# A two-layer perceiver on one core: another order of the first transfers and the first norm, and a feed-forward with one set of transposes and a written-out order

## The chip, the core and the metric

The kernel runs on one core of a Trainium2 chip, everything in 32-bit floats. The metric is device time in microseconds. One core has five engines with a program each: TensorE (PE; its weight loads are listed as PEld), VectorE (DVE), ScalarE (ACT), GpSimd (POOL) and SyncE (SP), whose queue issues nearly all transfers here. Engines wait for one another through semaphores; each works through its own program in order.

## The reference

The state `x` is 4 x 256 tokens of 256 numbers, the context 4 x 4096 rows of 256. Two layers, each a cross attention, a second block and a feed-forward:

```
x = x + L0_xattn(layernorm(x), ctx)     # scores times values, softmax over the 64 features of a head:
                                        #   no softmax over the keys, so keys and values enter as a gram matrix
x = x + L0_attn(layernorm(x))           # relative-position attention over the 4 batch entries, 16 heads
x = x + L0_ffn(layernorm(x))            # below
x = x + L1_xattn(layernorm(x), ctx, mask)   # softmax attention over 4096 masked keys
x = L1 self attention with rope and relu FFN, then L1 attention with 8 gated experts

def L0_ffn(u):                          # u = layernorm(x)
    experts(u, g, W1, b1, W2, b2) = gelu((u * rsqrt(mean(u*u) + eps) * g) @ W1 + b1) @ W2 + b2
    shared = sum of experts 0..1 on every token            # hidden size 1024
    scores = sigmoid(u @ centroids)                         # 8 routed experts
    gates, chosen = top_2(scores);  gates = gates / scores.sum()
    routed = sum over the two chosen of gate * expert
    return u + shared + routed
```

So after the feed-forward `x` has become x + u + shared + routed.

## The kernel before

`build` makes the constants, loads `x`, and then runs the blocks `l0_xattn`, `l0_attn`, `l0_ffn`, and the second layer, which the change leaves alone. The tokens lie as 8 tiles of 128 (`TT` = 8); `DC` = 2 is the width in units of 128, `FF` = 1024 the hidden size, `FC` = 8 the hidden size in units of 128, `NE` = 8 the routed experts. A `pool` hands out memory: a tile with a tag and `bufs=n` takes one of n buffers in turn and waits until the buffer's last reader is done. PSUM has 8 banks of 128 x 512; `mm_tile` takes one of three, `sc_tile` one of four in the feed-forward (`sc=(4, 1)`), `ps_o` has one. `contract` issues the matmuls of one product. A matmul in 32-bit floats appears as two records in the trace.

**Order.** Outside of a `manual_schedule()` a scheduler orders the instructions of a block by their dependences and estimated costs. Inside, each engine runs its instructions in the order in which the program states them. `l0_xattn` is written out in that way; `l0_ffn` isn't, up to its routed tiles.

**The start.** `Net.__init__` issues on SP the constants `cols` and `consts` and the mask; DVE turns the mask into additive numbers, `added`, and SP writes them to `away` in DRAM, where the second layer reads them. Then come `x`, and in `l0_xattn` chunk 0 of the context. The context goes through a ring of 4 chunks of 1 MB (`fetch`, 8 row tiles each, 4 chunks per batch entry); POOL sets a column of ones in each ring tile. `products(b, first, last)` adds up the gram matrix of batch entry b over its row tiles (lines 414 and 415). The written order is `products(0, 0, KC)`, the norm of `x` (`normed`, DVE: statistics at 240 and 241, an inverse root in 12 small operations at 183 to 190, `xn` at 247), 16 transposes on PE (`transposed`, line 263), 64 query matmuls, and then the batch entries one after another.

**The feed-forward, `l0_ffn`**, in the order of its text:

1. `normed` gives `u`, and `ms`, its mean square. `transposed` makes `uT`; 8 products of it with the centroids (`cs`) give the logits (line 812).
2. `score`, `top2` and the sums that make `chosen` and `gates` (line 827 and before it).
3. POOL adds `u` to `x`, tile by tile; `u` is multiplied by the inverse root of `ms` (line 827), and transposed a second time, with the shared gain, into `sT`.
4. `place` works out for each token its row in the list of slots of the routed experts: a `rank` product on PE (707, 708), a row of small DVE operations, one POOL operation (`part`, line 765, 1472 elements in each partition) and a reduction of it on DVE (line 769). Then 16 indirect transfers (line 832) scatter the tokens to `f0_rows` in DRAM.
5. For each of the 8 token tiles: the gates are transposed (`gT`, 839), copied by ACT (841), multiplied with the second biases `f0_b2` (843), and added to `x` by DVE (844).
6. For each of the 2 shared experts and each of 4 blocks of 256 tokens: the hidden layer `h`, where each f of `FC` is a product of two matmuls into half a PSUM bank, followed by ACT's gelu (867); f = 0 and 1 share a bank, 2 and 3 the next one, and so on. Then, for two tiles, the product with `w2` (`eo`, line 175 as all products of `contract`) and the add to `x` (872).
7. 23 tiles of routed slots, with the weights of the 8 routed experts (16 MB, `w1_all`, `w2_all`), which are loaded from the end of the attention on.

The loop of item 6, whose products and gelus the scheduler orders:

```
for f in range(FC):
    if f % 2 == 0:
        sc = self.sc_tile("h")[:, 0, :]
    part = sc[:, f % 2 * 256 : (f % 2 + 1) * 256]
    self.contract(part, [(w1[:, k, f * P : (f + 1) * P], sT[:, k, cols]) for k in range(DC)])
    nc.scalar.activation(h[:, f, :], part, AF.Gelu, bias=self.col("f0_b1", (NE + e) * FC + f))
```

Of the kernel before, what the change touches and what calls it, by code (L numbers as in the profile page):

```python
# [11 lines left out]
F32 = mybir.dt.float32  # L12
U8 = mybir.dt.uint8
# [5 lines left out]
P = 128  # L19
# [55 lines left out]
class Net:  # L75
    def __init__(self, ctx, tc, a, out):
# [14 lines left out]
        nc.sync.dma_start(self.cols, a["cols"])  # L91
        nc.sync.dma_start(self.consts, a["consts"])
        self.ones = self.const.tile([1, P], F32, name="ones")
        nc.vector.memset(self.ones, 1.0)

        self.away = tc.dram_tile([B, NK], F32, name="away")
        with tc.tile_pool(name="mask", bufs=1) as first:
            masked = first.tile([P, B * KC], U8, name="masked")
            nc.sync.dma_start(masked, a["mask"])
            added = first.tile([P, B * KC], F32, name="added")  # L100
            nc.vector.tensor_copy(added, masked)
            nc.vector.tensor_scalar(added, added, MASKED, None, ALU.mult)
            nc.sync.dma_start(self.away.rearrange("b (p k) -> (b p) k", k=B * KC), added)
        self.all_ones = self.const.tile([P, P], F32, name="all_ones")
        nc.vector.memset(self.all_ones, 1.0)

# [126 lines left out]
    def normed(self, x, out, tiles=range(TT), square=None):  # L233

        nc = self.nc
        n = len(tiles)
        stats = self.small.tile([P, n, 6], F32, tag="bn", name=self.name("bn"))
        mv = self.small.tile([P, n, 2], F32, tag="mv", name=self.name("mv"))
        for k, i in enumerate(tiles):
            nc.vector.bn_stats(stats[:, k, :], x[:, i, :])  # L240
            nc.vector.bn_aggr(mv[:, k, :], stats[:, k, :])
        rstd = self.rsqrt(mv[:, :, 1], EPS)
        if square is not None:
            nc.vector.tensor_mul(square, rstd, rstd)
            nc.vector.tensor_mul(square, square, mv[:, :, 1])
        for k, i in enumerate(tiles):
            nc.vector.tensor_scalar(
                out[:, i, :], x[:, i, :], mv[:, k, 0:1], rstd[:, k : k + 1], ALU.subtract, ALU.mult
            )
        return out  # L250
# [108 lines left out]
    def l0_xattn(self, x):  # L359
# [7 lines left out]
        with ExitStack() as ctx:  # L367
# [13 lines left out]

            fetch(0)
            fetch(1)
            wq = self.load_w(pool, "x0_wqT")
            fetch(2)

            brow = pool.tile([64, 512], F32, name="x0_brow")
            for j in range(2):
                nc.sync.dma_start(
                    brow[32 * j : 32 * j + 32, :], a["x0_qb"][:, j * 512 : (j + 1) * 512].partition_broadcast(32)  # L390
                )
            wo = self.load_w(pool, "x0_woT")
            ob = self.row("x0_ob")
# [3 lines left out]
            nc.vector.tensor_scalar(fixed[0], brow, rank[:64, 2:3], None, ALU.mult)  # L397
            nc.vector.tensor_scalar(fixed[1], brow, rank[:64, 0:1], None, ALU.mult)
# [120 lines left out]
            with self.tc.manual_schedule():  # L519
                products(0, 0, KC)  # L520
                xn = self.normed(x, self.tokens("xn"))
                xT = self.transposed(xn, "xT")
# [23 lines left out]
    def l0_attn(self, x):  # L546
# [3 lines left out]
        with ExitStack() as ctx:  # L550
# [6 lines left out]
            nc.sync.dma_start(bias, a["a0_bias"].partition_broadcast(P))  # L557

# [212 lines left out]

    def l0_ffn(self, x):
# [4 lines left out]
        with ExitStack() as ctx:  # L777
            pool = self.block(ctx, "f0", sc=(4, 1))
            rows = self.tc.dram_tile([SLOT_TILES * P, D], F32, name="f0_rows")
            results = self.tc.dram_tile([SLOT_TILES * P, D], F32, name="f0_results")  # L780
            cent = self.load_w(pool, "f0_cent")
            b2 = self.load(pool, "f0_b2", [NE + 2, D], a["f0_b2"])
            zero = pool.tile([P, D], F32, name="f0_zero")
            nc.gpsimd.memset(zero, 0.0)
            nc.sync.dma_start(
                rows.rearrange("(t p) d -> p t d", p=P), zero.unsqueeze(1).to_broadcast([P, SLOT_TILES, D])
            )
# [3 lines left out]
            ms = self.small.tile([P, TT], F32, tag="ms", name=self.name("ms"))  # L791
            u = self.normed(x, self.tokens("xn"), square=ms)
            w1_all, w2_all = (pool.tile([P, NE, DC * FF], F32, name=f"f0_w{n}_all") for n in (1, 2))
            with self.tc.tile_pool(name="f0_shared", bufs=1, reuse_waits="tile") as first:
                weights = {}

                def shared_weights(e):
                    weights[e] = (
                        self.load(first, "w1", [P, DC, FF], a["f0_W1_s"][e].rearrange("(k p) n -> p k n", p=P)),
                        self.load(first, "w2", [P, FC, D], a["f0_W2_s"][e].rearrange("(k p) n -> p k n", p=P)),  # L800
                    )

                shared_weights(0)
                uT = self.transposed(u, "xT", pool=first)
                score = first.tile([P, TT, NE], F32, name="f0_score")
                ps = self.mm_tile("cs")
                for i in range(TT):
                    self.contract(
                        ps[:, i * NE : (i + 1) * NE], [(uT[:, k, i * P : (i + 1) * P], cent[:, k, :]) for k in range(DC)]
                    )  # L810
                logit = first.tile([P, TT, NE], F32, name="f0_logit")
                nc.vector.tensor_copy(logit, ps[:, : TT * NE].rearrange("p (t e) -> p t e", e=NE))

                nc.scalar.activation(score, logit, AF.Exp, scale=-1.0)
                nc.vector.tensor_scalar(score, score, 1.0, None, ALU.add)
                nc.vector.reciprocal(score, score)
                nc.vector.tensor_copy(chosen, self.top2(score, logit, first))
                total = self.small.tile([P, TT], F32, tag="total", name=self.name("total"))
                nc.vector.tensor_reduce(total, score, AX.X, ALU.add)
                nc.vector.reciprocal(total, total)  # L820
                nc.vector.tensor_mul(score, score, chosen)
                nc.vector.tensor_mul(gates[:, :, :NE], score, total.unsqueeze(2).to_broadcast([P, TT, NE]))

                r = self.rsqrt(ms, EPS_RMS)
                for i in range(TT):
                    nc.gpsimd.tensor_add(x[:, i, :], x[:, i, :], u[:, i, :])
                    nc.vector.tensor_scalar(u[:, i, :], u[:, i, :], r[:, i : i + 1], None, ALU.mult)
                sT = self.transposed(u, "xT", "f0_gs", pool=first)
                slots, shares, where, bias = self.place(first, pool, chosen, gates[:, :, :NE])
                for side in range(2):  # L830
                    for i in range(TT):
                        nc.gpsimd.indirect_dma_start(
                            out=rows, out_offset=bass.IndirectOffsetOnAxis(ap=slots[:, side, i : i + 1], axis=0),
                            in_=u[:, i, :], in_offset=None,
                        )

                for i in range(TT):
                    ps = self.mm_tile("gT")
                    nc.tensor.transpose(ps[: NE + 2, :P], gates[:, i, :], self.ident)
                    gT = self.small.tile([NE + 2, P], F32, tag="gT", name=self.name("gT"))  # L840
                    nc.scalar.copy(gT, ps[: NE + 2, :P])
                    ps = self.mm_tile("b2")
                    nc.tensor.matmul(ps[:, :D], gT, b2, start=True, stop=True)
                    nc.vector.tensor_add(x[:, i, :], ps[:, :D], x[:, i, :])
                for e in range(2):
                    if e:
                        shared_weights(e)
                    w1, w2 = weights[e]
                    if not e:
                        for r in range(NE):  # L850
                            nc.sync.dma_start(
                                w1_all[:, r, :].rearrange("p (k n) -> p k n", k=DC),
                                a["f0_W1_r"][r].rearrange("(k p) n -> p k n", p=P),
                            )
                            nc.sync.dma_start(
                                w2_all[:, r, :].rearrange("p (k n) -> p k n", k=FC),
                                a["f0_W2_r"][r].rearrange("(k p) n -> p k n", p=P),
                            )
                    for n in range(4):
                        cols = slice(n * 256, (n + 1) * 256)  # L860
                        h = first.tile([P, FC, 256], F32, tag="h", name=self.name("h"), bufs=2)
                        for f in range(FC):
                            if f % 2 == 0:
                                sc = self.sc_tile("h")[:, 0, :]
                            part = sc[:, f % 2 * 256 : (f % 2 + 1) * 256]
                            self.contract(part, [(w1[:, k, f * P : (f + 1) * P], sT[:, k, cols]) for k in range(DC)])
                            nc.scalar.activation(h[:, f, :], part, AF.Gelu, bias=self.col("f0_b1", (NE + e) * FC + f))
                        for q in range(2):
# [950 lines left out]
```

## Time and profile before

| | us |
|---|---|
| median of 3 runs | 2364.1 (2363.99 to 2373.08) |
| the profiled execution | 2370.56 |
| its span, first to last instruction | 2368.8 |
| PE busy in the span | 2224.3 (94%) |
| start to the first gram product | 14.3 |
| norm of `x` in `l0_xattn`, PE idle | 8.1 |
| last `x` add of the attention to the first routed layer | 360.7 to 511.3 |
| second layer | from about 700 on |

Times in the trace count from the start of the span. "PEclk" is the share of full speed that TensorE was granted; at 0.5 a matmul takes twice as long. A line "A <- B: total, times, longest" says that A waited for B.

### The profile page before, as it was taken

What the parts mean: (1) busy time and instruction counts of PE and PEld (TensorE: products, weight loads), DVE (VectorE), ACT (ScalarE), POOL (GpSimd) and SP (SyncE); (2) the same over time, 40 slices, a digit from 0 to 9 for tenths busy, and PEclk for the clock granted to TensorE, in tenths of its full rate; (3) what the DMA queues carried; (4) which work ended last, traced back from release to release, by engine and by line L of the source; (5) the groups of instructions that cost most, each with busy time, mean ns of one, the idle gap of its engine ahead of it and who ended that gap; (6) DMA issues with size and microseconds to landing.
All of it is one profiled execution on the core that took longest, in us unless ns stands there. A gap on an engine that the chain in (4) does not pass through costs nothing.

```text
span 2368.8 us, 45856 instructions
## 1 busy us (share of the span) xinstructions
PE 2224.3 (94%) x19148; PEld 1339.5 (57%) x19148; DVE 1189.0 (50%) x2494; ACT 982.6 (41%) x1942; POOL 146.5 (6%) x270
## 2 busy tenths in 40 slices
PE   6999877999988999999999999999999899999996
PEld 4677535876752454455545554455554566666552
DVE  2333476012215766666666666665665176343545
ACT  0111111223333366655666556655555524344321
POOL 0000002100011000000000000000000042000121
PEclk9999866999999999999999999999999999999977
DMA  6121118101124112211121112210000120000000
GB/s 202 54 89 32 36 51 293 63 16 36 32 87 147 45 39 66 66 31 35 49 64 56 32 34 61 63 46 29 29 7 2 62 78 1 1 1 1 6 0 14
DMA packets 82432, 121.50 MB, mean 51 GB/s; under 512 B 5466, under 2 KB 52338, under 8 KB 82226
## 3 DMA queue, kind: packets, MB, share of 16 engines
q1 hardware_dynamic: 80690, 114.38, 15.4%
q0 software_dynamic: 1536, 4.20, 0.5%
q8 instruction: 151, 2.47, 0.4%
q14 instruction: 55, 0.45, 0.1%
HBM read 109.32 MB, written 9.24 MB: 50 GB/s over the span
## 4 chain that ended last, share of the span: by engine, by line
PE 87%; DVE 6%; issue 3%; ACT 2%; DMA 2%; SPq 0%; POOL 0%; POOLq 0%; DVEq 0%; ACTq 0%
PE sc L1092 14%; PE acc L1143 10%; PE mx L1105 9%; PE h L175 8%; PE v L1000 5%; PE k L1000 5%; PE ro L175 4%; PE we L175 3%; PE gram L414 2%; PE eo L175 2%; PE po L175 2%; PE sc L1560 2%; PE q L175 2%; PE xo L175 1%; PE qkv L175 1%
## 5 line engine op out<-in xcount | busy, mean ns | idle before, releaser
L1134 DVE TENSOR_REDUCE mx<-mx 128x1 f32<-128x512 f32 x988 | 636.6, 686 | 365.0 <-PE mx L1105 361.0
L1130 ACT ACTIVATE probs<-sc 128x512 f32<-128x512 f32 x988 | 536.8, 597 | 422.2 <-PE mx L1105 394.9
L1092 PE MATMUL sc<-qm,kT 32*128 32x256 f32 x3952 | 581.3, 401 | 8.9 <-ACT probs L1130 8.9
L1105 PE MATMUL mx<-kT,x_q 32*128 32x512 f32 x1976 | 561.1, 639 | 0.0
L1092 PEld LDWEIGHTS sc<-qm,kT 32*128 32x128 f32 x3952 | 352.3, 184 | 255.0 <-ACT probs L1130 129.3
L1143 PE MATMUL acc<-probs,v 128*32 128x256 f32 x4096 | 275.6, 386 | 0.0
L1143 PEld LDWEIGHTS acc<-probs,v 128*32 128x32 f32 x4096 | 107.3, 109 | 134.9 <-issue 90.1
L1105 PEld LDWEIGHTS mx<-kT,x_q 32*128 32x128 f32 x1976 | 150.9, 183 | 8.5 <-issue 7.2
L1000 PE MATMUL k<-slab,x_wk 128*32 128x512 f32 x1024 | 136.1, 618 | 11.8 <-DMA slab<-in_ctxT 10.9
L1000 PE MATMUL v<-x_wv,slab 128*32 128x256 f32 x2048 | 137.1, 385 | 0.0
L1574 DVE TENSOR_REDUCE negm<-mx 128x2 f32<-128x512 f32 x128 | 82.7, 686 | 94.8 <-PE mx L1566 92.9
L1572 ACT ACTIVATE probs<-sc 128x512 f32<-128x512 f32 x128 | 69.5, 595 | 136.1 <-PE mx L1566 93.9
L1566 PE MATMUL mx<-k,q 32*128 32x256 f32 x512 | 90.3, 435 | 24.5 <-DVE negm L1574 19.5
L309 ACT ACTIVATE kT<-k,cols 128x512 f32<-128x512 f32 x128 | 92.8, 783 | 23.2 <-PE k L1000 23.2
L346 POOL COPY wide<-rec 128x256 f32<-128x256 f32 x48 | 19.1, 398 | 1328.4 <-DVE rec L344 1317.0
L1000 PEld LDWEIGHTS v<-x_wv,slab 128*32 128x32 f32 x2048 | 53.4, 109 | 74.4 <-issue 46.3
L414 PE MATMUL gram<-x_ctx 128*128 128x257 f32 x256 | 79.2, 391 | 14.3 <-DMA x_ctx<-in_ctx 14.3
L1560 PE MATMUL sc<-qm,k 32*128 32x256 f32 x512 | 88.6, 439 | 0.0
L175 PE MATMUL h<-f_w_all,rT 128*128 x184 | 83.0, 594 | 0.7 <-DVE rT L888 0.6
L175 PE MATMUL ro<-f_w_all,hT 128*128 x368 | 83.3, 379 | 0.1
L912 ACT ACTIVATE hT<-hT,place 128x128 f32<-128x128 f32 x184 | 49.9, 383 | 77.8 <-PE hT L909 77.7
L175 PEld LDWEIGHTS ro<-f_w_all,hT 128*128 128x128 f32 x368 | 68.2, 190 | 9.1 <-issue 0.5
(365 smaller groups left out, 2664.4 us busy)
## 6 DMA issues: line engine op xcount, KB each, us to landing
slab<-in_ctxT SPq DMA_DIRECT2D x96, 512.0 KB
x_ctx<-in_ctx SPq DMA_DIRECT2D x16, 1024.0 KB
f_w_all<-in_f_W_r SPq DMA_DIRECT2D x16, 1024.0 KB
w<-in_f_W_s SPq DMA_DIRECT2D x4, 1024.0 KB
f_rows<-f_zero SPq DMA_DIRECT2D x1, 2944.0 KB
row<-f_rows SPq DMA_DIRECT2D x23, 128.0 KB
f_results<-y SPq DMA_DIRECT2D x23, 128.0 KB
kT<-away SPq DMA_DIRECT2D x128, 8.0 KB
```

What stands on the lines that cost most here:

```text
L175: nc.tensor.matmul(out, w, m, start=i == 0, stop=i == len(pairs) - 1)
L309: nc.scalar.activation(dst, ps, AF.Identity, bias=b, scale=own)
L414: nc.tensor.matmul(ps[:, : D + 1], t[:, :P], t, start=n == 0, stop=False)
L1000: nc.tensor.matmul(out[own], w[:, own], m, start=start, stop=not start, tile_position=(0, 32 * j))
L1092: nc.tensor.matmul(into[:, c * S : (c + 1) * S], kT[b, u, at // HALF][rows, at % HALF : at % HALF + P], qm[un][rows, :], start=True, stop= ...
L1105: nc.tensor.matmul(into, q[rows, b, u, t * P : (t + 1) * P], kT[b, u, at // HALF][rows, at % HALF : at % HALF + SLAB], start=True, stop=True,)
L1130: nc.scalar.activation(probs[j], sc[j], AF.Exp, scale=0.25)
L1134: nc.vector.tensor_reduce(mx[un2][:, k2 % 2, j, k2 // 2 : k2 // 2 + 1], bd[j], AX.X, ALU.max)
L1143: nc.tensor.matmul(acc[32 * j : 32 * j + 32, :S], v[b, chunk // VC][:, at : at + 32], probs[j][:, c * S : (c + 1) * S], start=k == 0 and c ...
L1560: nc.tensor.matmul(sc[j][:, c * S : (c + 1) * S], k[key][on_rows(j), u, c * P : (c + 1) * P], qm[i][on_rows(j), :], start=True, stop=True,)
L1566: nc.tensor.matmul(bd[j][:, c * S : (c + 1) * S], q[key][on_rows(j), u, c * P : (c + 1) * P], k[key][on_rows(j), u, :], start=True, stop=True,
L1574: nc.vector.tensor_reduce(negm[i2 % 2][:, :, 32 * j + UNIT_MAX[i2 % 2]], bd[j].rearrange("p (t s) -> p t s", s=S), AX.X, ALU.max, negate=True,
```

## The change

Three parts in one kernel.

1. **Start.** SP issues chunk 0 of the context first, then `x`, chunk 1, `cols`, `consts`, chunk 2 and `wq`. The norm stands in front of the first products; after a quarter of those, the text issues `brow`, `wo`, `ob` and the mask with its conversion (now a method, `mask`). The transposes follow the products as they did.
2. **Early loads.** A pool that lives through attention and feed-forward holds a zero tile, the centroids, `f0_b2`, and the first shared expert's `w1` and `w2`; `before_ffn` issues them and the filling of `f0_rows` with zeros (2944 KB) behind the attention's own weights.
3. **Feed-forward.** `u` is brought to its second scale at once (`by` = rstd times r), the logits are multiplied back by `back`. So one set of transposes serves both: DVE copies it to `uT`, ACT scales it into `sT`. The norm goes in two halves, the even tiles and the odd ones. ACT makes x + u as x * (1 + rstd) + shift. The shared experts are cut into `lower(e, n)` (the loop above) and `upper(e, n)` (the product with `w2`), and stand with the gates, `place`, the scatter and the `gT`/`b2` tiles in a written order. `place`'s `part` and the hidden layers take their buffers from the two tagged "h", as before, and `uT` now does so too; `gT` has three buffers, and `b2` goes to `ps_o`.

```diff
-        nc.sync.dma_start(self.cols, a["cols"])
-        nc.sync.dma_start(self.consts, a["consts"])
...
+            fetch(0)
+            nc.sync.dma_start(x, a["x"].rearrange("(t p) d -> p t d", p=P))
+            fetch(1)
+            nc.sync.dma_start(self.cols, a["cols"])
+            nc.sync.dma_start(self.consts, a["consts"])
+            fetch(2)
             wq = self.load_w(pool, "x0_wqT")
-            fetch(2)
...
             with self.tc.manual_schedule():
-                products(0, 0, KC)
                 xn = self.normed(x, self.tokens("xn"))
+                products(0, 0, 8)
+                for j in range(2):
+                    nc.sync.dma_start(brow[32 * j : 32 * j + 32, :], ...)
+                wo = self.load_w(pool, "x0_woT")
+                ob = self.row("x0_ob")
+                self.mask(pool)
+                nc.vector.tensor_scalar(fixed[0], brow, rank[:64, 2:3], None, ALU.mult)
+                nc.vector.tensor_scalar(fixed[1], brow, rank[:64, 0:1], None, ALU.mult)
+                products(0, 8, KC)
                 xT = self.transposed(xn, "xT")
...
+    def before_ffn(self):
+        nc, a = self.nc, self.a
+        self.f0_rows = self.tc.dram_tile([SLOT_TILES * P, D], F32, name="f0_rows")
+        zero = self.early.tile([P, D], F32, name="f0_zero")
+        nc.gpsimd.memset(zero, 0.0)
+        self.f0_cent = self.load_w(self.early, "f0_cent")
+        self.f0_b2 = self.load(self.early, "f0_b2", [NE + 2, D], a["f0_b2"])
+        self.f0_shared = {}
+        self.shared_weights(0)
+        nc.sync.dma_start(
+            self.f0_rows.rearrange("(t p) d -> p t d", p=P), zero.unsqueeze(1).to_broadcast([P, SLOT_TILES, D])
+        )
...
+                for half in range(2):
+                    tiles = range(half, TT, 2)
...
+                    nc.vector.tensor_mul(by, rstd, r)
+                    for k, i in enumerate(tiles):
+                        nc.vector.tensor_scalar(
+                            u[:, i, :], x[:, i, :], mv[:, k, 0:1], by[:, k : k + 1], ALU.subtract, ALU.mult
+                        )
...
+                    for c in range(DC):
+                        ps = self.mm_tile("tr")
+                        for k, i in enumerate(tiles):
+                            nc.tensor.transpose(ps[:, k * P : (k + 1) * P], u[:, i, c * P : (c + 1) * P], self.ident)
+                        ps = ps.rearrange("p (t n) -> p t n", n=P)
+                        nc.vector.tensor_copy(columns(uT, c, half), ps)
+                        nc.scalar.activation(columns(sT, c, half), ps, AF.Identity, scale=self.col("f0_gs", c))
...
+                    for k, i in enumerate(tiles):
+                        nc.scalar.activation(
+                            x[:, i, :], x[:, i, :], AF.Identity, bias=shift[:, k : k + 1], scale=keep[:, k : k + 1]
+                        )
+                nc.vector.tensor_tensor(logit, ..., back.unsqueeze(2).to_broadcast([P, TT, NE]), ALU.mult)
...
+                with self.tc.manual_schedule():
+                    nc.scalar.activation(score, logit, AF.Exp, scale=-1.0)
+                    lower(0, 0)
+                    nc.vector.tensor_scalar(score, score, 1.0, None, ALU.add)
...
+                    nc.vector.tensor_mul(gates[:, :, :NE], score, total.unsqueeze(2).to_broadcast([P, TT, NE]))
+                    lower(0, 1)
+                    upper(0, 0)
+                    lower(0, 2)
+                    slots, shares, where, bias = self.place(first, pool, chosen, gates[:, :, :NE])
+                    upper(0, 1)
+                    for side in range(2):
+                        for i in range(TT):
+                            nc.gpsimd.indirect_dma_start(out=rows, ...)
+                    upper(0, 2)
+                    lower(0, 3)
+                    upper(0, 3)
+                    self.shared_weights(1)
                     for i in range(TT):
                         ps = self.mm_tile("gT")
...
+                        ps = self.ps_o.tile([P, 512], F32, tag="o", name=self.name("b2"))
+                        nc.tensor.matmul(ps[:, :D], gT, b2, start=True, stop=True)
+                        nc.vector.tensor_add(x[:, i, :], ps[:, :D], x[:, i, :])
+                    lower(1, 0)
                     for n in range(4):
+                        if n < 3:
+                            lower(1, n + 1)
+                        upper(1, n)
...
+        x = net.l0_xattn(x)
+        with ExitStack() as ffn:
+            net.early = ffn.enter_context(tc.tile_pool(name="f0_early", bufs=1, reuse_waits="tile"))
+            x = net.l0_attn(x)
+            x = net.l0_ffn(x)
```

## The prediction

> **What bounds the kernel now.** I read five views, in this order: the page's busy shares, the windows by stage, the waits of the first 60 us, the chain that ended last, and the order of instructions around the shared experts.
>
> ```profile
> PE 2224.3 (94%) x19148; PEld 1339.5 (57%) x19148; DVE 1189.0 (50%) x2494; ACT 982.6 (41%) x1942; POOL 146.5 (6%) x270
> PE 87%; DVE 6%; issue 3%; ACT 2%; DMA 2%; SPq 0%; POOL 0%; POOLq 0%; DVEq 0%; ACTq 0%
> ```
>
> TensorE is busy for 94% of the span and is 87% of the chain. The DVE share and the DMA share (8% together) are where a reordering can win; anything that leaves PE waiting where it is now dense loses at once. The windows show where it is dense (window and its length, PE, PEld, DVE, ACT, POOL busy, granted PE clock, DMA share, GB/s):
>
> ```profile
> 0.00:14.30 14.30, 0.02 (x1) 0.06 (x1) 0.76 (x4) 1.28 (x1) 2.68 (x12) 1.00 0.66 195
> 38.40:46.50 8.10, 0.03 (x1) 0.00 (x0) 7.01 (x33) 0.27 (x1) 0.00 (x0) 0.64 0.42 132
> 360.70:407.50 46.80, 35.36 (x125) 24.53 (x126) 33.32 (x110) 7.60 (x19) 12.02 (x11) 0.60 1.03 364
> 407.50:511.30 103.80, 103.80 (x482) 89.70 (x481) 6.37 (x15) 26.98 (x57) 13.43 (x14) 1.00 0.14 44
> ```
>
> PE stands still for 14.3 us at the start and for 8.1 us while DVE normalises. The feed-forward's head (360.7 to 407.5) is thin and at a clock of 0.60. Its shared experts (407.5 to 511.3) have no hole: 15 blocks of 6.92 us, eight `lower` and seven `upper` (the first `lower` lies in the head). The waits name the two early holes (engine, waited for: total, times, longest):
>
> ```profile
> PE gram L414 <- DMA x_ctx<-in_ctx: 14.3, 1, 14.3
> PE tr L263 <- DVE xn L247: 8.1, 1, 8.1
> POOL x_ctx L372 <- DMA away<-added: 6.8, 1, 6.8
> ```
>
> The third says why the first is so long (POOL's memset in the ring waits for the same transfer): chunk 0 of the context is issued at 8.08, after the mask has been loaded, converted and written to `away`.
>
> **Part A, the start.** The trace has chunk 0 issued at 8.08 and landed at 14.14 (6.06), `x` issued at 2.13 and landed by 7.8 (5.7 at most, 5.1 at least). Chunk 0 now goes out first, at the 0.74 of today's first transfer: it lands at 5.8 to 6.8, and the first `gram` moves from 14.28 to 6.0-6.9: -7.5. Behind it, at the 2.9 to 3.0 us per MB of the streaming stretch, come `x` (9.6) and chunks 1, 2 and 3 (12.6, 16.2, 22.3; two columns of constants and `wq` lie between). PE eats a chunk in 5.24 us at full clock, twice that at half, and needs them at about 14, 19.5 and 24.5. None is late, by 1 us at the least; `brow`, `wo`, the mask and `away` land by 27 and are wanted from 38 on. The norm then lies under the products: -8.1, and the 16 transposes behind it no longer run at half clock (4.09 against about 2.4): -1.7. Sum -17.3; from -15 (a chunk 1 us late and a warm-up of one clock window more) to -19.
>
> **Part B, the early loads.** 5 MB are issued ahead of the attention on SP. In the built order the attention's own weights now wait for context chunks 2 and 3 of batch 3 (about 213 and 219, today's times) and not 0 and 1; they land by about 226 and are wanted from 269 on. The expert's weights land by 240, for use at 380. All covered by the last batch's PE work: 0. If that cover were gone, the price would be one load, 6 us.
>
> **Part C, the feed-forward**, from the last `x` add (360.7) to the first routed layer (511.3), 150.6 us now: 26.1 to the first `h` (386.8), then 124.5 for 16 blocks of 6.92 (110.7) and 13.8 of gating work (gate transposes, `b2`, the rank, half clock).
>
> C1, head. Half 0's statistics are done under the last tiles. Afterwards DVE has 7 small operations (0.2 each), four `xn` (0.345), two copies from PSUM (0.6 each), then 26 small operations for half 1 (5.2), four more `xn` (1.4), PE's last transposes 0.7, two copies 1.2, and 8 `cs` products (3.5 at half clock, from 6.83 for 32 records): 18.9 with their waits. The first `h` moves from +26.1 to +18.9: -7.2 (-4 to -9). Gone with it are 8 POOL adds, the second 16 transposes (3.90) and the top-2 chain, which now lies under `lower`.
>
> C2, the new wait. `lower` is written f = 0, 1, 2...; two f share a PSUM bank. In the built order PE's first matmul for each odd f waits for ACT's gelu of the even f before it: four waits in each of eight `lower`, 32. Today's order has the same dependence, but the scheduler put another bank's products between. The timeline shows the price (start, length, engine, work):
>
> ```profile
> 414.24 4.05 PE L175 MATMUL h<-xT,w 128*128 128x256 f32 x18
> 415.31 0.47 ACT L867 ACTIVATE h<-h,cols 128x256 f32<-128x256 f32 x1 [7.30 <-PE h L175]
> 416.17 0.47 ACT L867 ACTIVATE h<-h,cols 128x256 f32<-128x256 f32 x1 [0.39 <-PE h L175]
> 399.76 0.47 ACT L867 ACTIVATE h<-h,cols 128x256 f32<-128x256 f32 x1
> 400.29 0.50 PEld L175 LDWEIGHTS h<-xT,w 128*128 128x128 f32 x2 [0.55 <-ACT h L867]
> ```
>
> One f is 0.866 of PE; gelu begins 0.21 behind its end (414.24+0.87 to 415.31), takes 0.47, and PE goes on 0.05 later (400.23 to 400.29) with a weight load uncovered (0.24, estimated from a routed product whose 16 records take 3.73 behind a wait and 3.46 without one). Sum 0.97, at least 0.74 without the weight load: 32 x 0.97 = +31.0 (23.7 to 32). The first gelu has the logits' exp (0.26) and the table load (1.28, seen at 398.47) ahead of it on ACT; both end about when the first f does at half clock. No other PE work is queued between: PE follows program order.
>
> C3, `gT` and `b2`. Eight tiles now stand in a row between `upper(0, 3)` and `lower(1, 0)`, nothing between them. Today a tile with one `h` pair takes 1.3 us at full clock and 1.9 at half, of which PE's own part is 0.9; alone it is a chain PE, ACT (0.25), PE (0.69), DVE (0.41) of about 1.27. At full clock 8 tiles are 10.2, at half 15.2. Which clock?
>
> ```profile
> 392.25:395.67 3.42, 3.42 (x15) 1.65 (x15) 3.04 (x20) 0.51 (x2) 0.00 (x0) 1.00 1.08 361
> 395.67:399.08 3.41, 3.01 (x7) 1.34 (x7) 2.97 (x11) 1.12 (x3) 2.81 (x2) 0.50 1.03 386
> 399.08:402.49 3.41, 3.15 (x7) 1.09 (x5) 3.41 (x4) 2.36 (x6) 2.75 (x2) 0.50 1.08 378
> ```
>
> In 392.25 to 395.67 PE was never idle, and the clock halved behind it: `b2` uses 10 of the array's 128 rows. Weighting each matmul by its rows, that stretch streams 0.44 of the time; others at 0.51 and 0.56 kept full clock, and half clock ended behind 0.38. Eight tiles with no `h` among them stream less, so about one 3.4-us stretch runs at full and the rest at half: 13 (10.2 to 15.2, or 8 if tiles overlap). The next `lower` starts at half, as does the first: +5 for both (2 to 9).
>
> [...]
>
> C4, `part`. It shares the two buffers named "h" with `uT` and the hidden layer, and so waits for `upper(0, 1)`; POOL takes 3.91, DVE's reduction 1.67, and behind that on DVE stands the `x` add that frees the PSUM tile of `upper(0, 2)`'s second half. PE has 3.46 of work meanwhile and stops for about 4 minus what overlaps: +4 taken (2 to 6; 0 if POOL starts early). The rank adds 0.5. The 16 scatters (2.67 apart) end by about 480, the second expert's weights have 17 us of `upper` and `b2` before them: 0 both. Routed tiles and the whole second layer keep their order on every engine: 0.
>
> Sum of C: -7.2 -13.8 +31.0 +13 +5 +4 +0.5 = +32.5. With A: +15.2. The profiled execution (2370.6, of which 2368.8 span) is 6.5 above the median of 2364.1; differences carry over, so 2364.1 + 15.2 = **2379**. All ends added, A and C give -8 to +30: 2356 to 2394.
>
> **Rivals.**
> 1. The waits of C2 are not paid, because gelu's end is in time or PE passes on by columns: C is +1.5, the whole -15.8, 2348. Against it: the row at 400.29, where PE waits for a gelu of the same bank, and the built order. It decides where a stall costs under 0.49 (0.97 less 15.2 / 32). [...] Chance 0.10.
> 2. The clock halves inside the stalled `lower`. With 0.97 lost in 2.70, a 3.4-us stretch streams between 0.51 and 0.72 of the time, just above the 0.44 that halved. A `lower` at half costs 17.9 and not 10.7; four of eight is +29: 2408. Chance 0.10.
> 3. A does not come: the transfers run beside one another, chunk 0 lands with `x` and chunk 1 at 10 to 12, and half of the gain goes: 2388. For it: four transfers issued within 2 us share the same queues. Against: today chunk 0 lands 3.0 before chunk 1. Chance 0.07.
>
> **Chances.** A measurement of this kernel can tell about 0.5% (11.8 us) from no change, so the bounds are 2352.3 and 2375.9. Main case 0.73: about a third of it below 2375.9, nearly none below 2352.3. Rival 1 is faster for 0.07 and the same for 0.03; rivals 2 and 3 are slower. Faster 0.09, same 0.28, slower 0.63. The range reaches up past the main case for part of rival 2, and cuts off rival 1: 2357 to 2397.
>
> **What would show it.** First `gram` at 6 to 7 and no wait of 8 us for `xn`; 32 waits "PE h <- ACT h" of 0.7 to 1.0; a `lower` of 10.7; eight `b2` with no `h` between at a clock below 1; about 4 us of PE waiting for the `x` add; the same work from the first routed tile on. A `lower` near 7 makes the prediction wrong downwards, near 18 upwards.

## The result, and the profile after

| | before | changed |
|---|---|---|
| median, 14 runs each (us) | 2370.55 | 2387.86 |
| ratio | | 1.0061, 95% interval 1.0048 to 1.0075 |
| profiled execution, its span | 2370.56, 2368.8 | 2383.12, 2381.3 |
| first gram product | 14.28 | 6.95 |
| end of the query products | 78.31 | 60.43 |
| last `x` add of the attention | 360.73 | 342.54 |
| first routed layer | 512.04 | 526.77 |

The kernel became 0.6% slower: 14 us by the ratio (11 to 18 by its interval); the two medians differ by 17.3. By the last `x` add of the attention it is 18.2 ahead; it loses 32.9 between there and the first routed layer (184.2 against 151.3), and is 14.7 behind. (The 511.3 given ahead for the kernel before is the end of the shared experts' products; the first product of the routed layer follows 0.7 later.) The shares of busy time of the changed kernel show nothing of this:

```profile
PE 2235.5 (94%) x19132; PEld 1340.5 (56%) x19132; DVE 1188.8 (50%) x2518; ACT 988.5 (42%) x1952; POOL 140.4 (6%) x262
```

The windows of the changed kernel, with the columns of those shown before: the start, the head with the first `lower`, the row of gate tiles, the next `lower`, and the one behind it.

```profile
0.00:6.95 6.95, 0.00 (x1) 0.03 (x1) 0.31 (x2) 1.28 (x1) 2.62 (x12) 1.00 0.68 210
342.50:375.20 32.70, 25.70 (x80) 19.62 (x81) 16.09 (x64) 11.62 (x21) 0.00 (x0) 0.53 1.04 370
437.60:450.52 12.92, 9.77 (x26) 3.83 (x24) 3.40 (x8) 2.03 (x8) 3.60 (x4) 0.68 0.37 122
450.52:467.01 16.49, 14.23 (x33) 9.47 (x33) 0.42 (x1) 3.32 (x7) 4.79 (x5) 0.53 0.11 40
467.01:477.50 10.49, 8.23 (x35) 5.99 (x34) 0.00 (x0) 3.78 (x8) 0.00 (x0) 1.00 0.00 0
```

Where before had 103.8 us without a hole there are now holes at full clock (8.23 of 10.49 busy) and, at the head of each expert, half clock (0.53). The changed kernel's waits between the last `x` add and the first routed layer name the holes (engine, waited for: total, times, longest):

```profile
PE h L175 <- ACT h L884: 19.3, 32, 1.3
PE b L927 <- ACT gT L925: 3.1, 8, 0.4
PE eo L175 <- DVE x L892: 3.1, 1, 3.1
```

The timeline of the changed kernel shows one of the 32 (start, length, engine, work, idle time before it):

```profile
396.64 2.00 PE L175 MATMUL h<-f_sT,w 128*128 128x256 f32 x8 [0.56 <-ACT h L884]
397.81 0.47 ACT L884 ACTIVATE h<-h,cols 128x256 f32<-128x256 f32 x1 [1.22 <-PE h L175]
398.67 0.47 ACT L884 ACTIVATE h<-h,cols 128x256 f32<-128x256 f32 x1 [0.39 <-PE h L175]
399.20 1.99 PE L175 MATMUL h<-f_sT,w 128*128 128x256 f32 x8 [0.56 <-ACT h L884]
```

An odd f and the next even one (8 records) take 2.00, then PE stands for 0.56 while ACT applies the gelu of the even one. From start to start it is 2.56, for work of 1.73.

### The profile page after: what moved, and what is told of

The parts are those of the page before. It is cut to its first block, busy times and chain, and to the rows that moved or that the text cites. A ratio compares the mean times of both kernels' runs of the same rounds, so it can differ in the third digit from the quotient of the medians.

```text
span 2381.3 us, 45848 instructions
## 1 busy us (share of the span) xinstructions
PE 2235.5 (94%) x19132; PEld 1340.5 (56%) x19132; DVE 1188.8 (50%) x2518; ACT 988.5 (42%) x1952; POOL 140.4 (6%) x262
## 3 DMA queue, kind: packets, MB, share of 16 engines
q1 hardware_dynamic: 80690, 114.38, 15.2%
## 4 chain that ended last, share of the span: by engine, by line
PE 87%; DVE 6%; issue 3%; ACT 2%; DMA 2%; SPq 0%; POOL 0%; POOLq 0%; DVEq 0%; ACTq 0%
PE sc L1153 14%; PE acc L1204 10%; PE h L175 9%; PE mx L1166 9%; PE v L1061 5%; PE k L1061 5%; PE ro L175 4%; PE we L175 3%; PE gram L407 2%; PE po L175 2%; PE sc L1621 2%; PE eo L175 2%; PE q L175 2%; PE xo L175 1%; PE qkv L175 1%
## 5 line engine op out<-in xcount | busy, mean ns | idle before, releaser
L343 POOL COPY wide<-rec 128x256 f32<-128x256 f32 x48 | 19.1, 398 | 1327.8 <-DVE rec L341 1316.5
L175 PE MATMUL h<-f_sT,w 128*128 128x256 f32 x256 | 78.0, 451 | 19.4 <-ACT h L884 19.3
```

The source lines that it names most:

```text
L175: nc.tensor.matmul(out, w, m, start=i == 0, stop=i == len(pairs) - 1)
```

## The experiments

"Stretch" is the time from the attention's last `x` add to the first routed layer: 151.3 before, 184.2 after. Whole times carry the noise of the unchanged second layer (last section), so kernels are compared by the stretch, from one profile of each. A ratio is given where a kernel was run four or five times, against seven or eight runs of the kernel before on the same chip; `interleaved`, `gates_between`, `own_part`, `scheduled` and the two kernels with a wider `b2` were run once.

**The two halves apart.** `start_only` takes the new transfers and norm with the old feed-forward and no early loads; `ffn_only` the old start with the early loads and the new feed-forward.

```diff
 start_only, against the changed kernel (l0_ffn and normed with the text of before)
-            self.before_ffn()
...
-            net.early = ffn.enter_context(tc.tile_pool(name="f0_early", bufs=1, reuse_waits="tile"))
 ffn_only, against the kernel before (l0_ffn with the text of the change)
+            self.before_ffn()
...
+            net.early = ffn.enter_context(tc.tile_pool(name="f0_early", bufs=1, reuse_waits="tile"))
```

> The new order of the first transfers and of the first norm alone; feed-forward and early loads as before. Theory: the start is worth 17 to 18 us and nothing later takes it back, so about 2353 against 2370.6, and the end of the query products moves from 78 to 60-61. Rival (part of the gain is lost again before the second layer, since the scatter and loads behind it do not move along): 2358 to 2364.

> The early loads and the new feed-forward alone, with the start as before. Theory: the whole loss is here, +31 to +34, about 2403; last x add of the attention to first routed layer 183 to 185 against 151. Rival (part of the loss belongs to the earlier start, whose transfers press on the attention's): below +28.

`start_only`: ratio 0.9916 (0.9883 to 0.9948); first gram product 6.70, query products done at 60.52, last `x` add 342.91, and the profiled span is 17.9 shorter: nothing takes it back. The whole gain is there, and with it the 8.1 of waiting for `xn` are gone. `ffn_only`: ratio 1.0113 (1.0084 to 1.0142), stretch 180.2, that is +28.9: below the 31 to 34 expected and just above the rival's 28. By the ratio the loss is 27 us (20 to 34), too wide to decide. Its clock is at half for 44 us of the stretch and not 55, because the second half-clock phase ended after 13.6 instead of 23.9; that is worth some 4 us (an estimate), the whole difference to the changed kernel. Whether the earlier start moves the clock or chance does, one profile can't tell.

**The 32 waits.** `own_bank` gives each f its own PSUM bank, `interleaved` keeps two to a bank and takes two banks in turn.

```diff
 own_bank
-    if f % 2 == 0:
-        sc = self.sc_tile("h")[:, 0, :]
-    part = sc[:, f % 2 * 256 : (f % 2 + 1) * 256]
+    part = self.sc_tile("h")[:, 0, :256]
 interleaved
+    for f0 in range(0, FC, 4):
+        banks = [self.sc_tile("h")[:, 0, :] for _ in range(2)]
+        for f in (f0, f0 + 2, f0 + 1, f0 + 3):
+            part = banks[f % 4 // 2][:, f % 2 * 256 : (f % 2 + 1) * 256]
```

> The changed kernel, with a PSUM bank for each f of the hidden layer instead of one for two; the written order stays. Theory: the 32 waits of 0.83 go (-26.6), and since the first lower of each expert then streams twice as densely, the clock comes back earlier there (-5 to -9): 2352 to 2356, a lower of 6.9. Rival 1 (the waits are not by bank, or ACT cannot keep up in the written order): no change, 2386 to 2390. Rival 2 (the waits go, but the half-clock stretches stay): -27, about 2361.

> The changed kernel, with two f to a bank as it is, but the products of two banks taken in turn (f = 0, 2, 1, 3). Theory: same as a bank for each f, -32 to -36, since a wait of 0.73 lies under a product of 0.87. Rival (it is the sharing of the bank that costs, not the order): the waits stay and the time does.

`own_bank`: ratio 0.9919 (0.9889 to 0.9949), stretch 147.7; `interleaved`: stretch 148.0. Both take away 36.2 to 36.5, and neither has any of the 32 waits left. So the waits need both, the shared bank and the order that takes its two products one after the other; with either one changed there are none. The timeline of `own_bank` at the start of its second `lower`:

```profile
363.76 8.58 PE L175 MATMUL h<-f_sT,w 128*128 128x256 f32 x39
365.04 0.47 ACT L882 ACTIVATE h<-h,cols 128x256 f32<-128x256 f32 x1 [0.39 <-PE h L175]
365.90 0.47 ACT L882 ACTIVATE h<-h,cols 128x256 f32<-128x256 f32 x1 [0.39 <-PE h L175]
```

And from the chain that ended last of `interleaved` (start, length, work), 52 records in one piece:

```profile
362.65 11.45 PE h L175 x52
```

In `own_bank` PE runs 39 records without a hole, and now ACT waits, 0.39 before each gelu. 26.6 of the 36.5 are the waits (32 x 0.83). The rest is clock: 30.7 us at half instead of 54.6, and the two `lower` that begin at half lose some 4.6 us by it instead of 14.2.

**The row of gate tiles.** `gates_between` puts the `gT` and `b2` of two tiles between the products of each of the second expert's `lower`: `gate(i, 0)` is the transpose of tile i and its copy, `gate(i, 1)` the product with `b2` and the add.

```diff
                 def lower(e, n):
...
                         nc.scalar.activation(h[:, f, :], part, AF.Gelu, bias=self.col("f0_b1", (NE + e) * FC + f))
+                        if e and f % 2:
+                            gate(2 * n + f // 4, f // 2 % 2)
...
-                    for i in range(TT):
-                        ps = self.mm_tile("gT")
...
```

> The changed kernel, with the eight tiles of gate transposes and b2 put between the products of the second expert's four lower instead of in a row before them. Theory: the row of 12.9 goes, of which 4 to 6 come back as PE's own work (some of it under the waits for the gelu), the clock stays at full in the first lower of the second expert (16.5 becomes 10.3): -13 to -17. Rival (the clock halves there for the waits, not for the row of b2): -7 to -9, and the half-clock stretch only moves.

Stretch 172.1, -12.1, just short of the 13 to 17. The window of the second expert's first `lower`, gate tiles included:

```profile
437.60:449.66 12.06, 9.74 (x40) 6.09 (x38) 0.85 (x2) 4.06 (x10) 3.50 (x4) 1.00 0.36 120
```

The second half-clock phase is gone (30.7 us at half, all in the head), while the 32 waits are still there (19.1 us in total). So the row of gate tiles made it, and not the waits; the rival falls. The row and the slow `lower` behind it (12.9 and 6.5 too many) went; by difference 7.3 came back as gate work between products, which fits four `lower` of 12.06 instead of 10.2.

**PE's stop in `upper(0, 2)`.** The prediction laid it on `part`'s shared buffer. `own_part` gives `part` a buffer of its own, in two pieces.

```diff
-        part = pool.tile(each, F32, tag="h", name=self.name("part"), bufs=2)
...
+        for lo, hi in ((0, 12), (12, SLOT_TILES)):
+            each = [P, hi - lo, FC, NE]
+            part = pool.tile([P, 12, FC, NE], F32, tag="part", name=self.name("part"), bufs=1)[:, : hi - lo]
...
```

> The changed kernel, with the operation for the biases (part) in a buffer of its own, in two pieces, instead of one of the two named h. Theory: it no longer waits for upper(0, 1), runs under it, and PE's stop of 3.4 us in upper(0, 2) goes: -3 to -4. Rival (the stop comes from the chain of small operations before it, which ends at about the same time): -0 to -1.

Stretch 183.4 (-0.8), the size that the rival gave. The clock has a part in that number: `own_part` has one more 3.4 us at half clock, right behind the stop, and a second half-clock phase that is shorter by 6.8. So the timelines decide. That of the changed kernel around the stop:

```profile
410.71 3.93 POOL L769 TENSOR_TENSOR part<-place,cols 128x1472 f32<-128x1472 f32 x1 [105.92 <-DVE place L762]
410.73 3.94 DVE L764 CAST place<-place 128x23 int32<-128x23 f32 x1
414.67 1.69 DVE L773 TENSOR_REDUCE place<-part 128x184 f32<-128x1472 f32 x1
416.28 1.07 DVE L892 TENSOR_TENSOR x<-eo,x 128x256 f32<-128x256 f32 x3
416.75 3.72 PE L175 MATMUL eo<-w,h 128*128 128x256 f32 x16 [3.05 <-DVE x L892]
```

And two lines from the timeline of `own_part`, `part`'s first piece and the product behind the stop:

```profile
408.94 2.15 POOL L771 TENSOR_TENSOR part<-place,cols 128x768 f32<-128x768 f32 x1 [105.71 <-DVE place L758]
415.42 5.41 PE L175 MATMUL eo<-w,h 128*128 128x256 f32 x16 [3.35 <-DVE x L893]
```

The stop is still there, 3.35 instead of 3.05 (the product behind it takes 5.41 and not 3.72 because it runs at half clock). POOL waits in both for DVE's small operations and for no buffer. These run from the rank product (402.7) to 410.7; `upper(0, 1)` is done at about 410.0, so its buffer was not what came last. PE waits for the `x` add that stands on DVE behind the whole of `place`. If that order is the cause, it is enough to state `place` earlier, where DVE has nothing to do. `all_three` joins own banks, own part and gates between; `early_place` is `all_three` with one line moved:

```diff
     upper(0, 0)
+    slots, shares, where, bias = self.place(first, pool, chosen, gates[:, :, :NE])
     lower(0, 2)
-    slots, shares, where, bias = self.place(first, pool, chosen, gates[:, :, :NE])
```

> The changed kernel with a PSUM bank for each f, the part in its own buffer, and the gate tiles between the second expert's products. Theory: the effects add, less what they share (the clock of the second expert's first lower is counted twice): -45 to -50, about 2338 to 2343, and faster than the kernel before by 27 to 32. Rival (they uncover one another's waits): -35 or less.

> The written order with a bank for each f, the part in its own buffer and the gate tiles between, and now with place stated before lower(0, 2) and not behind it. Theory: PE's stop of 3.4 in upper(0, 2) comes from the x add that stands on DVE behind place's chain of some 35 small operations; that chain now runs under lower(0, 2), so the stretch goes from 141.2 to 137 to 138, level with the scheduler's. Rival (the stop comes from part or its buffer): 140 to 141.

`all_three`: stretch 141.2, that is -43.0: short of the 45 to 50 expected, beyond the rival's 35. Its ratio to before is 0.9888 (0.9863 to 0.9913), 27 us faster; its median of 2348.1 is above the 2338 to 2343 expected. The stop remains in its waits:

```profile
PE eo L175 <- DVE x L904: 3.4, 1, 3.4
```

`early_place`: 137.6, as expected, and this wait is gone. One line was moved, so the order on DVE is shown as the cause. Whether `part` needs its own buffer once `place` stands earlier was not run. The ratio is 0.9865 (0.9839 to 0.9890).

**No written order.** `scheduled` has the text of the changed feed-forward and leaves the order to the scheduler.

```diff
-                with self.tc.manual_schedule():
+                with ExitStack():
```

> The changed kernel with the feed-forward's written order taken away: the same text, ordered by the scheduler as before. Theory: the scheduler puts another bank's products between and the gate tiles among them as it did, so the stretch from the last x add to the first routed layer is that of before less the shorter head: 138 to 148 against 184, time -36 to -46. Rival (one set of transposes is itself what costs): 160 or more.

> The kernel with the new start and one set of transposes, and the feed-forward ordered by the scheduler, now timed. Its stretch from the last x add to the first routed layer was 137.8 against 151.3 before, and the start is worth 18: theory -31 to -32 against before, a ratio of 0.986 to 0.988. Rival (the rest of the kernel takes some of it back): above 0.990.

Stretch 137.8 and 137.7: without the written order the new feed-forward gains 13.6 on the kernel before, and the written order cost 46.5. The 13.6 belong to one set of transposes and all that came with it (the norm in halves, ACT's add, the early loads), which were not run apart. The timed ratio is 0.9883 (0.9851 to 0.9915), a little above the 0.986 to 0.988 expected; its interval reaches past the rival's 0.990 too. In the chain that ended last (`scheduled`; start, length, work) a gate tile lies between products of `h`:

```profile
416.94 0.22 PE gT L923 x2
417.15 0.43 PE h L175 x2
417.59 0.62 PE b L927 x2
```

`scheduled`, `early_place` and `all_three` are the fastest here, 27 to 32 us under the kernel before; their intervals overlap and their whole times are not told apart.

**What the clock goes by.** Both kernels widen `b2` to 512 columns, on 10 or on 112 rows of the array (`WIDE_K`). The added numbers are zeros. The gates get `WIDE_K` columns as well, so their transposes (`gT`) use 10 or 112 columns of the array.

```diff
+        self.f0_b2 = self.early.tile([WIDE_K, 512], F32, name="f0_b2")
...
-            nc.tensor.matmul(ps[:, :D], gT, b2, start=True, stop=True)
+            nc.tensor.matmul(ps, gT, b2, start=True, stop=True)
```

> The changed kernel with the b2 product widened to 512 columns (the added ones are zeros that nobody reads), still on 10 of the array's 128 rows. A tile of the gate stage then has about 1.7 us at full clock, 1.1 of it streaming. Theory (the clock goes by columns streamed, weighted by the rows in use): the clock halves within the stage, which takes 17 to 20, and the next lower takes about 16.5. Rival (it goes by whether TensorE is streaming or idle): full clock, the stage 13.6, the next lower 10.3.

> The same widened product, with gates and b2 filled up with zeros to 112 rows: the same number of instructions and columns, other rows. Theory: the stage streams about 0.55 of the time by that weight and stays at full clock: 13 to 14, the next lower 10.3, so the feed-forward is 8 to 12 shorter than with 10 rows. Rival: no difference between the two.

The windows of the gate stage and of what follows it, with 10 rows:

```profile
437.50:456.57 19.07, 15.92 (x26) 4.02 (x24) 3.40 (x8) 2.03 (x8) 5.87 (x7) 0.62 0.29 96
456.57:473.20 16.63, 13.68 (x44) 9.37 (x44) 0.43 (x1) 4.82 (x11) 2.55 (x3) 0.82 0.07 24
```

And with 112 rows:

```profile
437.01:450.54 13.53, 9.69 (x26) 3.67 (x25) 3.40 (x8) 2.13 (x8) 3.72 (x5) 1.00 0.39 116
450.54:460.70 10.16, 7.90 (x33) 5.67 (x33) 0.42 (x1) 3.32 (x7) 3.70 (x4) 1.00 0.14 52
```

There are 26 matmul records in each stage. With 10 rows the clock is 0.62 and the stage takes 19.1; with 112 it never leaves full speed and takes 13.5. The stretch is 186.7 against 178.4. In the 3.4 us before the clock fell with 10 rows, columns streamed for 0.55 of the time, and in a like stretch with 112 rows for 0.56; weighted by the rows in use that is 0.10 against 0.50 (estimates, at the about 0.21 us that an `h` record takes for 256 columns). So in this pair streaming alone did not set the clock. The pair does not tell the rows of `b2` from the columns of `gT`, since both went from 10 to 112. The `lower` behind 10 rows recovered sooner than expected (13.1 instead of 16.5).

## Why the prediction was right, point by point

The forecast was +15.2 for the whole, by the sum -17.3 and +32.5; measured are +14 (ratio 1.0061), -18.2 and +32.9. The forecast time, 2379, is 9 below the measured median of 2387.9; 6.5 of that is its base, 2364.1 from three runs of the kernel before, where 14 runs give 2370.55. The terms are less good than their sum:

| term | predicted | measured |
|---|---|---|
| A, start | -17.3 | -17.9 at the end of the query products |
| C1, head | -7.2 | -11.1 |
| gating work of before | -13.8 | -13.8, read off the kernel before |
| C2, 32 waits | +31.0 | +26.6 |
| C3, row of gate tiles | +13 | +12.9 |
| half clock in the two first `lower` | +5 | +14.2 |
| C4, stop | +4 | +3.4 |
| rank | +0.5 | +0.4 |

Part A held, to where its chunks arrive: no PE wait for the context behind the first. The first product comes 7.3 earlier, the 8.1 of waiting for `xn` are gone, and about 2.4 are left for the transposes and the warm-up (at first two `gram` records of 128x257 take 0.86 together and not 0.43, up to about 20.2 before and 12.2 after), where the prediction had 1.7. Part B cost nothing that `start_only` and the changed kernel, 60.5 and 60.4 at the query products and 342.9 and 342.5 at the last `x` add, could show.

C1 was mis-sized, outside of its bounds: the head, without the 1.22 of `h` that went ahead of `cs`, took 15.0 and not 18.9. Of the seven small operations put behind the last add, all but about 0.5 us were done before it (it ends at 342.54, the first `xn` starts at 343.46), which is 0.9 of the difference. The terms that the prediction names add up to 16.0; the 2.9 that it adds as "their waits" did not come on top.

C2 had the right mechanism and count, with 0.83 for a wait and not 0.97. The idle time is 0.56 and the 8 records take 2.00 instead of 1.73, together 0.83. The end of these 2.00 (398.64) lies only 0.03 ahead of the gelu (398.67): most of the 0.21 between a product's end and its gelu is already in the longer records, and was counted a second time beside the 0.24 of the weight load (whose own rows, 3.73 and 3.46, differ by 0.27). The prediction's list of 15 dense blocks is turned round: the kernel before has seven `lower` and eight `upper` there, since the first `lower` lies in the head; no term uses that.

The half clock was the worst term: +14.2 (17.9 and 16.7 for two `lower`, against 10.2 for the others), where the bounds ended at 9. The prediction let it end after a stretch or two. With the waits in it, though, a `lower` at half clock streams, by the prediction's weighting, some 0.32 to 0.45 of each 3.4-us stretch (an estimate, from 0.216 a record, 1.73 for 8, at full clock), around the 0.38 behind which the prediction saw the clock come back. Here it came back behind 0.45 in one `lower` and 0.40 in the other, which stayed at half for 16 us (450.5 to 466.1). Of the 17.9, about 0.8 is the gelu table's load (1.28 on ACT at 359.46; PE's first wait for a gelu is 1.34 and not 0.56). That is rival 2 in small: not inside a `lower` at full clock, which never fell, but in one that begins at half. C1's and C2's errors (-8.3 together) and this one (+9.2) cancel; that the sum was hit to half a microsecond is luck.

C3 came out at its size (12.9 against 13), and the pair with 10 and 112 rows bears its reason out. The rival recorded for the pair, full clock in both, falls: PE never stood still for longer than 0.5 us in either stage (in all 3.15 of 19.07 with 10 rows, 3.84 of 13.53 with 112), and with 10 rows the clock halved all the same (0.62 over the stage). Idle time of PE did not decide it here.

C4 had the size (3.05 of waiting, 3.4 with the slower first product behind it) and the end of the chain, the `x` add behind the reduction. Its start was wrong, as `own_part` and `early_place` show: `part` waits for DVE's small operations and not for the shared buffer.

Rival 1 falls with the 32 waits in the trace. Rival 3 falls with `start_only`: chunk 0 landed for a first product at 6.7, and PE waited for no later chunk.

## What to carry to other kernels

A written order fixes the products as the text states them: where two results shared a PSUM bank, the second product waited for the first one's reader (19.3 us of idle time over the 32, none with another bank's product between), and these waits, with the half clock that they drew out, cost 36 us here. The whole written order cost 46 and ate a change that was worth some 31 (18 at the start, 13.6 in the feed-forward). Before replacing a scheduler's order, list each engine's waits in the built order and price each by the work queued behind it. A small operation (a bias product, a bookkeeping chain) was cheap between large products and dear in a row of its own, where the bias products also cost the clock of what followed: the gate tiles cost 7.3 us between products and 19.4 in a row, and `place` stated earlier took 3.6 off.

## What the runs showed of the hardware

- **The clock fell with few rows of the array in use, though PE was never idle for longer than 0.5 us.** With the same number of products and of columns streamed, 10 rows brought the clock to half (0.62 over the stage), and 112 kept it at 1.00; one run of each. Whether rows alone count, or the share of the array in use, is open.
- **A cast on DVE lasted as long as the POOL operation beside it.** The cast of 23 elements in each partition at 410.73 took 3.94, beside POOL's `part` of 3.93, where the operation of the same shape just before it took 0.18; in `own_part` the same cast took 2.02 beside a POOL operation of 2.15. It ends 0.03 and 0.04 behind POOL's operation (414.67 against 414.64, 411.13 against 411.09). What ties the two engines was not shown.
- **The unchanged second layer isn't constant.** From its first context product to the end it took between 1664 and 1682 in 14 profiles on several chips, by the same order of instructions on DVE and ACT. `own_part` with 2398.3 looks 10 us worse than the changed kernel, and its stretch is shorter. The clock is part of the spread: the time at half clock in that layer goes from 116 to 156 us, 127 in the kernel before (1666) and 156 in `own_part` (1682). It isn't all of it: `scheduled` has 128 and took 1677. What moves the clock there stays open.
